# A timetable by single products, tile steps in two halves, and attention rows in pairs

## The chip, the core and the metric

The kernel runs on one core of a Trainium2 chip. Its time is the device time of one execution in microseconds (us), as the median of several runs. Less is better. The core has a matrix engine (TensorE, PE in the profile, with its weight loads as PEld), a vector engine (VectorE, DVE), a scalar engine (ScalarE, ACT), GpSimd (POOL) and SyncE (SP). Each engine works through its own list of instructions in order; the engines wait for each other by semaphores. Transfers are issued from the lists of SP and of POOL and then run on 16 DMA engines that all share.

## The reference

One layer on 2048 tokens of 512 channels: x plus an RWKV attention plus a mixture of experts, both on the normalised x.

```python
x = L0_attn_x                                   # [1, 2048, 512]
xn = _layernorm(x)
x = x + attn(xn) + ffn(xn)

# attn
rvk = einsum('btc,dc->btd', xn, W_rvk)
r, v, k = split(rvk, 3)
y = sigmoid(r) * wkv(time_decay, time_first, k, v)     # scan over time, state (p, q, o) per channel
out = einsum('btc,dc->btd', y, W_out)

# ffn
probs = softmax(einsum('bsh,eh->bse', xn, classifier_w))        # 12 experts, 8 real, 4 that pass x on
idx = top_k(probs + bias, 2); w_full = probs at idx * 1.5
act = silu(xn @ gate_w[e].T) * (xn @ up_w[e].T)                 # INTER = 256
out = sum over e < 8 of w_full[e] * (act @ down_w[e].T) + xn * (sum of w_full[8:])
```

## The kernel before

**Data.** The 2048 tokens are 4 blocks of 512 (`NTB`, `TB`), each of 4 rows of 128 tokens (`NJ`). The channels are 4 groups of 128 (`CC`). A *unit* (b, c) of the attention is one block in one group: three groups of four products (k, v, r; `project`, L259), each group accumulated in one PSUM bank of `ps_mm` and copied by ScalarE to a tile, and then a scan along time (`scan`, L282) on VectorE in four stages, with two exps on ScalarE between the first and the second stage and a reciprocal in the last. A *product* here is one 128x128 by 128x512 matrix product in fp32. When a block's four units are through, its four *attention rows* follow (`attention`, L719): four products with the output weight into one bank, one VectorE add of x's share (L740) onto a row read back from `xs` (`read_xn`, L697), and an accumulating store from POOL into `out` (L743). The normalised x lies in the DRAM tensor `xs`; `out` was filled with x at the start.

**The experts.** Tokens are sorted by expert into 25 *tiles* of 128 places. A tile i takes:

- `gather(i)`: POOL fetches 128 rows of `xs` into xg (two buffers).
- `fetch(i)`, `fetch_down(i)`: SP loads the expert's up weights (gw, 1 MB, three buffers) and down weights (dw, three buffers).
- `flip(i)`: ScalarE copies xg into 16-bit halves (xp, one buffer), SP issues a DMA that transposes them (xq). `unite(i)`: ScalarE joins the halves to xgT. So the transpose is done without TensorE.
- `up(i)`: four products into a bank of `ps_gu`. `activate(i)`: a tanh on ScalarE, two VectorE operations; the result is act.
- `flip_act(i)`, `unite_act(i)`: the same detour for act, by way of ap and aq, one buffer each, to actT. The last two tiles transpose act on TensorE instead (`turn_act`).
- `finish(i)`: two down products into a bank of `ps_o` (two banks), ScalarE scales them into yo (three buffers), and POOL adds them into `out` by an indirect transfer.

**The order.** It is written out by hand (`tc.manual_schedule`): each engine gets its instructions in the order in which the program calls them. Up to unit 3 the program is a fixed sequence. From L770 on it is a *timetable*: a list of entries (time, number of steps, generator), sorted by time and then run through. The times are units of a plan, not measurements. `total` = 44 groups * 3.43 + 25 tiles * 5.2 = 280.9. The 44 groups are 36 of the projections and 8 attention rows of blocks 0 and 1 (`after`, L772). Group m stands at `total * m / groups`, all four products at once. The scan stages of unit u stand at (u - 1) * 19 + 0, 4, 6 and 12. Tile step i stands at 6 + 10.68 i, whole. `read_xn` of a row comes 16 before its group, its add 3 after the group.

`step(i, n)` (L669) calls, in this order: fetch i+2; unite_act i-2; flip_act i-1; up i; activate i; gather i+3; finish i-2; flip i+2; fetch_down i+1; unite i+1. In the last step turn_act and finish of tile i-1 are called too.

After the timetable block 2's rows are read (into places of the four-buffer pool `base`, like rows 0 to 7) and block 3's rows (into one place of the gw weights), and block 2's attention rows follow. Then comes a branch that holds a loop for further tiles, which isn't entered with this data, and the rows of block 3, which add to rows of `out` that are read back (`read_out`).

Rows are numbered i = 4 b + j below. Before the change rows 0 to 7 accumulate in banks of `ps_o`, together with the tiles' down products, and of block 2 every second row in `ps_mm`.

Of the kernel before, what the change touches and what calls it, by code (L numbers as in the profile page):

```python
# [26 lines left out]
F32 = mybir.dt.float32  # L27
# [8 lines left out]
P = 128  # L36
T = 2048
C = 512
CC = C // P
TB = 512  # L40
NTB = T // TB
NJ = TB // P
# [9 lines left out]
TILES = 25  # L52
# [7 lines left out]
def layer(ctx: ExitStack, tc: tile.TileContext, x, w_rvk, w_out, decay, first, cls, ebias, gu, down, out):  # L60
    nc = tc.nc

    def pool(name, bufs, **kw):
        return ctx.enter_context(tc.tile_pool(name=name, bufs=bufs, **kw))
# [18 lines left out]
    ps_tr = pool("ps_tr", 2, space=bass.MemoryType.PSUM)  # L83
# [412 lines left out]
    for m in range(2):  # L496
# [21 lines left out]
        for j in range(NT):  # L518
            k = m * NT + j
# [33 lines left out]
    def gather(i, token=token_i):  # L553

        xg = gathered.tile([P, C], F32, tag="xg", name=f"xg{i}")
        nc.gpsimd.indirect_dma_start(  # L556
            out=xg,
            out_offset=None,
            in_=xs,
            in_offset=bass.IndirectOffsetOnAxis(ap=token[:, i : i + 1], axis=0),  # L560
        )
        st[i] = {"xg": xg}

    def fetch(i, which=which_i):

        e = nc.values_load(
            which[0:1, i : i + 1],
            engines=(SP,),
            min_val=0,
            max_val=E - 1,  # L570
            skip_runtime_bounds_check_because="a sum of E - 1 comparisons",
        )
        w = ewp.tile([P, CC, 2 * INTER], F32, tag="gw", name=f"gw{i}")
        nc.sync.dma_start(w, gu[bass.ds(e, 1)].rearrange("o p c n -> p (o c) n"))
        st[i].update(w=w, e=e)

    def fetch_down(i):
        d = ewp.tile([P, IC, C], F32, tag="dw", name=f"dw{i}")
        nc.sync.dma_start(d, down[bass.ds(st[i]["e"], 1)].rearrange("o p c n -> p (o c) n"))
        st[i]["d"] = d  # L580
# [10 lines left out]
    def flip(i):  # L591

        xp = wk1.tile([P, 2, C], U16, tag="xp", name=f"xp{i}")
        nc.scalar.copy(xp, st[i]["xg"].bitcast(U16).rearrange("p (c h) -> p h c", h=2))  # L594
        xq = ex_p.tile([P, 2 * CC, P], U16, tag="xq", name=f"xq{i}")
        nc.sync.dma_start_transpose(xq, xp.rearrange("p h c -> p (h c)"))
        st[i]["xq"] = xq

    def unite(i):

        xgT = ex_p.tile([P, CC, P], F32, tag="xgT", name=f"xgT{i}")
        nc.scalar.copy(  # L602
            xgT.bitcast(U16).rearrange("p c (t h) -> p c t h", h=2),
            st[i]["xq"].rearrange("p (h c) t -> p c t h", h=2),
        )
        st[i]["xgT"] = xgT

    def up(i, cs):

        if 0 in cs:  # L610
            st[i]["pg"] = ps_gu.tile([P, 2, INTER], F32, tag="gu", name=f"pg{i}")
        pg = st[i]["pg"]
        for c in cs:
            nc.tensor.matmul(  # L614
                pg, st[i]["xgT"][:, c, :], st[i]["w"][:, c, :], start=(c == 0), stop=(c == CC - 1)
            )

    def activate(i):
        pg = st[i]["pg"]

        th = ex_p.tile([P, INTER], F32, tag="th", name=f"th{i}")
        nc.scalar.activation(th, pg[:, 0, :], AF.Tanh, scale=0.5)  # L622
        nc.vector.scalar_tensor_tensor(th, th, 1.0, pg[:, 0, :], ALU.add, ALU.mult)  # L623
        act = ex_p.tile([P, INTER], F32, tag="act", name=f"act{i}")
        nc.vector.tensor_mul(act, th, pg[:, 1, :])
        st[i]["act"] = act

    def turn_act(i):
        pt = ps_tr.tile([P, IC, P], F32, tag="tr", name=f"pa{i}")
        for c in range(IC):  # L630
            nc.tensor.transpose(pt[:, c, :], st[i]["act"][:, c * P : (c + 1) * P], ident)
        actT = ex_p.tile([P, IC, P], F32, tag="actT", name=f"actT{i}")
        nc.scalar.copy(actT, pt)
        st[i]["actT"] = actT

    def flip_act(i):

        ap = wk1.tile([P, 2, INTER], U16, tag="ap", name=f"ap{i}")
        nc.scalar.copy(ap, st[i]["act"].bitcast(U16).rearrange("p (c h) -> p h c", h=2))
        aq = wk1.tile([P, 2 * IC, P], U16, tag="aq", name=f"aq{i}")  # L640
        nc.sync.dma_start_transpose(aq, ap.rearrange("p h c -> p (h c)"))
        st[i]["aq"] = aq

    def unite_act(i):
        actT = ex_p.tile([P, IC, P], F32, tag="actT", name=f"actT{i}")
        nc.scalar.copy(  # L646
            actT.bitcast(U16).rearrange("p c (t h) -> p c t h", h=2),
            st[i]["aq"].rearrange("p (h c) t -> p c t h", h=2),
        )
        st[i]["actT"] = actT  # L650
# [15 lines left out]
        )  # L666
        del st[i]

    def step(i, n):  # L669

        if i + 2 < n:
            fetch(i + 2)
        if i > 1:
            unite_act(i - 2)
        if 0 < i < n - 1:
            flip_act(i - 1)
        up(i, (0, 1))
        if i == n - 1:
            turn_act(i - 1)
        up(i, (2, 3))  # L680
        activate(i)
        if i + 3 < n:
            gather(i + 3)
        if i > 1:
            finish(i - 2)
        if i == n - 1:
            finish(i - 1)
        if i + 2 < n:
            flip(i + 2)
        if 2 <= i + 1 < n:  # L690
            fetch_down(i + 1)
        if i + 1 < n:
            unite(i + 1)

    xrows, orows = {}, {}

    def read_xn(b, js=range(NJ)):  # L697
        if b == NTB - 1:
            t = ewp.tile([P, NJ, C], F32, tag="gw", name=f"xrows{b}")
        for j in js:  # L700
            i = b * NJ + j
            if b == NTB - 1:
                xrows[i] = t[:, j, :]
            else:
                xrows[i] = basep.tile([P, C], F32, tag="base", name=f"xrow{i}")
            nc.sync.dma_start(xrows[i], xs[i * P : (i + 1) * P, :])
# [12 lines left out]
    def attention(b, js=range(NJ)):  # L719

        for j in js:
            i = b * NJ + j
            if j >= 2 if i in orows else b == NTB - 2 and j % 2 == 1:
                po = ps_mm.tile([P, C], F32, tag="mm", name=f"pw{i}")
            else:
                po = ps_o.tile([P, C], F32, tag="o", name=f"pw{i}")
            for c in range(CC):
                nc.tensor.matmul(  # L728
                    po,
                    yT[b][:, c, j * P : (j + 1) * P],  # L730
                    wout_sb[:, c, :],
                    start=(c == 0),
                    stop=(c == CC - 1),
                )
            yield
            if i in orows:
                nc.vector.tensor_add(orows[i], orows[i], po)  # L737
                nc.sync.dma_start(out[i * P : (i + 1) * P, :], orows[i])
            else:
                nc.vector.scalar_tensor_tensor(  # L740
                    xrows[i], xrows[i], zw[:, i : i + 1], po, ALU.mult, ALU.add
                )
                nc.gpsimd.dma_start(out[i * P : (i + 1) * P, :], xrows[i], accum_op=ALU.add)  # L743
            yield


    gather(0)
# [5 lines left out]
    stages = [scan(*u) for u in units]  # L753
# [15 lines left out]

    UNIT = 19.0  # L770
    ahead = [p for p in [project(*u) for u in units[LEAD:]] for _ in range(3)]
    after = {14: (0, 0), 17: (0, 1), 20: (0, 2), 23: (0, 3), 34: (1, 0), 37: (1, 1), 40: (1, 2), 43: (1, 3)}  # L772
    groups = len(ahead) + len(after)
    total = groups * 3.43 + TILES * 5.2
    table = []
    for u in range(1, len(units)):
        for k, at in enumerate((0, 4, 6, 12)):
            table.append(((u - 1) * UNIT + at, 1, stages[u]))
    for m in range(groups):
        at = total * m / groups  # L780
        if m in after:
            b, j = after[m]
            table.append((at - 16, 1, iter([(read_xn, b, [j])])))
            row = attention(b, [j])
            table += [(at, 1, row), (at + 3, 1, row)]
        else:
            table.append((at, CC, ahead.pop(0)))


    spread = (total - 14) / TILES  # L790
    for i in range(TILES):
        table.append((6 + spread * i, 1, iter([(step, i, TILES)])))
    table.append((6 + spread * TILES, 1, iter([(turn_act, TILES - 1)])))
    table.append((9 + spread * TILES, 1, iter([(finish, TILES - 1)])))
    for _, n, work in sorted(table, key=lambda entry: entry[0]):
        for _ in range(n):
            todo = next(work, None)
            if todo:
                todo[0](*todo[1:])
    read_xn(NTB - 2)  # L800
    read_xn(NTB - 1)
    whole(attention(NTB - 2))
    manual.close()

# [69 lines left out]
```

## Time and profile before

| | |
|---|---|
| three runs | 395.91, 396.14, 403.66 us (median 396.14) |
| profiled execution | 394.85 us, span from first to last instruction 393.1 us |
| TensorE clock granted | 1.0 throughout |
| first TensorE instruction | 9.63 us after the span's start |
| DMA | 88.80 MB, mean 226 GB/s |

The page's second part shows 40 slices of the span, each digit the busy share in tenths:

```profile
PE   0999999999999999999999999999999999999995
DVE  5872898997866648677666493976857658857405
ACT  2765112554464555636344644655563455332000
POOL 4002001421041333312233240423331311223300
DMA  8998907465789869879999999799899898843694
```

Of the costliest groups these belong to the tiles and rows of the timetable. Columns: line, engine, operation, output <- inputs, shape, count | busy us, mean ns of one | idle time of the engine just before them, with what ended most of it.

```profile
L614 PE MATMUL pg<-gw,xgT 128*128 128x512 f32 x200 | 90.1, 592 | 0.0
L728 PE MATMUL pw<-wout_sb,yT 128*128 128x512 f32 x128 | 57.0, 594 | 0.9 <-ACT yo L659 0.8
L323 DVE RECIPROCAL den<-den 128x512 f32<-128x512 f32 x16 | 53.5, 3344 | 0.0
L655 PE MATMUL po<-dw,actT 128*128 128x512 f32 x100 | 46.9, 593 | 1.0 <-ACT actT L646 1.0
L602 ACT COPY xgT<-xq 128x1024 uint16<-128x1024 uint16 x25 | 29.0, 1160 | 0.0
```

A busy time is a sum over the records of one group. Idle time counts only on the engine that is the bound; elsewhere it costs nothing by itself.

### The profile page before, as it was taken

The numbers are of one execution on the slowest core, as the hardware profiler recorded it, in microseconds if no ns is written. First come the engines' busy times: TensorE is split into PE (matmuls) and PEld (weight loads), VectorE is DVE, ScalarE is ACT, GpSimd is POOL, SyncE is SP. The second block draws the span as 40 slices with busy tenths as digits, with TensorE's granted clock in tenths as the row PEclk, the third lists the DMA queues.
The fourth block names the chain that finished last, engine by engine and source line by source line (L and its number), as shares of the span: only waits on it lengthen the run. The fifth ranks groups of instructions, "written<-read, shape, count | busy, mean of one in ns | idle before, by whom it ended". The sixth has DMA issues, their size and how long they took to land. (4 is left out here: it accounts for less than half of the span.)

```text
span 393.1 us, 3511 instructions
## 1 busy us (share of the span) xinstructions
PE 374.8 (95%) x994; PEld 169.6 (43%) x994; DVE 271.1 (69%) x397; ACT 170.5 (43%) x278; POOL 98.8 (25%) x130
## 2 busy tenths in 40 slices
PE   0999999999999999999999999999999999999995
PEld 0545445444444434444444444444444444444432
DVE  5872898997866648677666493976857658857405
ACT  2765112554464555636344644655563455332000
POOL 4002001421041333312233240423331311223300
PEclk9999999999999999999999999999999999999999
DMA  8998907465789869879999999799899898843694
GB/s 265 412 392 329 321 28 320 113 177 164 217 220 245 252 155 249 209 227 272 276 260 210 207 261 236 212 263 278 244 262 261 235 208 238 200 64 46 89 258 162
DMA packets 62885, 88.80 MB, mean 226 GB/s; under 512 B 42192, under 2 KB 42320, under 8 KB 59088
## 3 DMA queue, kind: packets, MB, share of 16 engines
q1 hardware_dynamic: 55328, 67.85, 57.1%
q0 software_dynamic: 7536, 20.71, 26.8%
q8 instruction: 8, 0.13, 0.1%
q14 instruction: 13, 0.11, 0.1%
HBM read 63.78 MB, written 19.40 MB: 212 GB/s over the span
## 5 line engine op out<-in xcount | busy, mean ns | idle before, releaser
L614 PE MATMUL pg<-gw,xgT 128*128 128x512 f32 x200 | 90.1, 592 | 0.0
L660 POOL DMA_INDIRECT out_dram<-yo,to_i x25 | 43.3, 1731 | 134.2 <-ACT yo L659 79.7
L265 PE MATMUL pk<-xnT,wrvk 128*128 128x512 f32 x128 | 58.9, 596 | 0.0
L614 PEld LDWEIGHTS pg<-gw,xgT 128*128 128x128 f32 x200 | 37.9, 190 | 47.4 <-issue 45.4
L728 PE MATMUL pw<-wout_sb,yT 128*128 128x512 f32 x128 | 57.0, 594 | 0.9 <-ACT yo L659 0.8
L265 PE MATMUL pr<-xnT,wrvk 128*128 128x512 f32 x128 | 57.7, 592 | 0.0
L265 PE MATMUL pv<-xnT,wrvk 128*128 128x512 f32 x128 | 57.6, 593 | 0.0
L323 DVE RECIPROCAL den<-den 128x512 f32<-128x512 f32 x16 | 53.5, 3344 | 0.0
L309 DVE TENSOR_TENSOR_SCAN sums<-obv,state,a 128x512 f32<-128x512 f32 x16 | 20.5, 1283 | 40.2 <-ACT obv L303 40.2
L655 PE MATMUL po<-dw,actT 128*128 128x512 f32 x100 | 46.9, 593 | 1.0 <-ACT actT L646 1.0
L556 POOL DMA_INDIRECT xg<-xs,token_i x25 | 30.1, 1205 | 43.4 <-DVE empty L543 27.4
L623 DVE SCALAR_TENSOR_TENSOR th<-th,pg 128x256 f32<-128x256 f32 x25 | 10.5, 419 | 41.0 <-ACT th L622 41.0
L728 PEld LDWEIGHTS pw<-wout_sb,yT 128*128 128x128 f32 x128 | 24.0, 190 | 32.0 <-issue 29.6
L265 PEld LDWEIGHTS pv<-xnT,wrvk 128*128 128x128 f32 x128 | 24.2, 190 | 30.1 <-issue 29.9
L265 PEld LDWEIGHTS pr<-xnT,wrvk 128*128 128x128 f32 x128 | 24.2, 190 | 30.1 <-issue 30.1
L265 PEld LDWEIGHTS pk<-xnT,wrvk 128*128 128x128 f32 x128 | 23.7, 190 | 31.2 <-issue 30.6
L659 ACT ACTIVATE yo<-po,wplace 128x512 f32<-128x512 f32 x25 | 17.2, 687 | 35.1 <-PE po L655 35.1
L655 PEld LDWEIGHTS po<-dw,actT 128*128 128x128 f32 x100 | 18.9, 190 | 25.2 <-issue 22.5
L622 ACT ACTIVATE th<-pg 128x256 f32<-128x256 f32 x25 | 9.6, 384 | 45.7 <-PE pg L614 45.6
L602 ACT COPY xgT<-xq 128x1024 uint16<-128x1024 uint16 x25 | 29.0, 1160 | 0.0
L594 ACT COPY xp<-xg 128x1024 uint16<-128x1024 uint16 x25 | 25.9, 1038 | 6.3 <-DMA xq<-xp 3.5
L743 POOL DMA_DIRECT2D out_dram<-xrow x12 | 11.1, 1007 | 56.9 <-DMA out_dram<-yo,to_i 45.5
(151 smaller groups left out, 368.3 us busy)
## 6 DMA issues: line engine op xcount, KB each, us to landing
gw<-in_gu_dram SPq DMA_DIRECT2D x25, 1024.0 KB, 7.5
dw<-in_down_dram SPq DMA_DIRECT2D x25, 512.0 KB, 5.5
x<-in_x_dram SPq DMA_DIRECT2D x16, 256.0 KB, 5.2
xs<-x SPq DMA_DIRECT2D x16, 256.0 KB, 5.0
wrvk<-in_w_rvk_dram SPq DMA_DIRECT2D x3, 1024.0 KB, 7.2
xrow<-xs SPq DMA_DIRECT2D x12, 256.0 KB, 5.2
out_dram<-xrow POOLq DMA_DIRECT2D x12, 256.0 KB, 5.9
wout_sb<-in_w_out_dram SPq DMA_DIRECT2D x1, 1024.0 KB, 10.1
```

Of the source, the lines that this page charges most:

```text
L265: nc.tensor.matmul(ps, wrvk_sb[m][:, k, c * P : (c + 1) * P], xnT[b][:, k, :], start=(k == 0), stop=(k == CC - 1),)
L309: nc.vector.tensor_tensor_scan(sq, bs, a2, s[:, 3:4], ALU.add, ALU.mult)
L323: nc.vector.reciprocal(den, den)
L556: nc.gpsimd.indirect_dma_start(out=xg, out_offset=None, in_=xs, in_offset=bass.IndirectOffsetOnAxis(ap=token[:, i : i + 1], axis=0),)
L594: nc.scalar.copy(xp, st[i]["xg"].bitcast(U16).rearrange("p (c h) -> p h c", h=2))
L602: nc.scalar.copy(xgT.bitcast(U16).rearrange("p c (t h) -> p c t h", h=2), st[i]["xq"].rearrange("p (h c) t -> p c t h", h=2),)
L614: nc.tensor.matmul(pg, st[i]["xgT"][:, c, :], st[i]["w"][:, c, :], start=(c == 0), stop=(c == CC - 1))
L655: nc.tensor.matmul(po, st[i]["actT"][:, c, :], st[i]["d"][:, c, :], start=(c == 0), stop=(c == IC - 1))
L659: nc.scalar.activation(yo, po, AF.Identity, scale=weight[:, i : i + 1])
L660: nc.gpsimd.indirect_dma_start(out=out, out_offset=bass.IndirectOffsetOnAxis(ap=to[:, i : i + 1], axis=0), in_=yo, in_offset=None, compute ...
L728: nc.tensor.matmul(po, yT[b][:, c, j * P : (j + 1) * P], wout_sb[:, c, :], start=(c == 0), stop=(c == CC - 1),)
L743: nc.gpsimd.dma_start(out[i * P : (i + 1) * P, :], xrows[i], accum_op=ALU.add)
```

## The change

The timetable's entries become single calls. A helper `plan(at, what, *args)` adds an entry; a group's four products are planned one by one, `one` = 280.9 / 44 / 4 = 1.596 apart, instead of four at one time, so that other work can stand between them. `attention` yields after each product accordingly, and its add is the fifth call.

`step` is cut into `first_half` (fetch i+2, flip_act i-1, up i, activate i, unite_act i-2, gather i+3) and `second_half` (unite i+1, flip i+2, finish i-2, fetch_down i+1), planned 0.6 of a step later. So unite_act moves behind activate, and unite ahead of flip and finish.

The rows of blocks 0 and 1 stand in pairs of neighbouring groups (14, 15; 20, 21; 34, 35; 42, 43), and both adds of a pair come at one time behind the pair's products. Rows 0 to 5 accumulate in banks of `ps_tr`, row 6 in `ps_o`, row 7 in `ps_mm`. Block 2's rows are read into a weight place (tag gw) as block 3's were, and both reads are entries of the timetable, near its end.

```diff
-    def step(i, n):
+    def first_half(i, n):
         if i + 2 < n:
             fetch(i + 2)
-        if i > 1:
-            unite_act(i - 2)
         if 0 < i < n - 1:
             flip_act(i - 1)
         up(i, (0, 1))
...
         up(i, (2, 3))
         activate(i)
+        if i > 1:
+            unite_act(i - 2)
         if i + 3 < n:
             gather(i + 3)
+
+    def second_half(i, n):
+        if i + 1 < n:
+            unite(i + 1)
+        if i + 2 < n:
+            flip(i + 2)
         if i > 1:
             finish(i - 2)
         if i == n - 1:
             finish(i - 1)
-        if i + 2 < n:
-            flip(i + 2)
         if 2 <= i + 1 < n:
             fetch_down(i + 1)
-        if i + 1 < n:
-            unite(i + 1)
...
     def read_xn(b, js=range(NJ)):
-        if b == NTB - 1:
+        if b >= NTB - 2:
             t = ewp.tile([P, NJ, C], F32, tag="gw", name=f"xrows{b}")
...
-            if j >= 2 if i in orows else b == NTB - 2 and j % 2 == 1:
+            if i < (NTB - 2) * NJ - 2:
+                po = ps_tr.tile([P, C], F32, tag="tr", name=f"pw{i}")
+            elif j >= 2 if i in orows else j % 2 == 1:
                 po = ps_mm.tile([P, C], F32, tag="mm", name=f"pw{i}")
             else:
                 po = ps_o.tile([P, C], F32, tag="o", name=f"pw{i}")
...
-            yield
+                yield
...
-    after = {14: (0, 0), 17: (0, 1), 20: (0, 2), 23: (0, 3), 34: (1, 0), 37: (1, 1), 40: (1, 2), 43: (1, 3)}
+    after = {14: (0, 0), 15: (0, 1), 20: (0, 2), 21: (0, 3), 34: (1, 0), 35: (1, 1), 42: (1, 2), 43: (1, 3)}
+    def plan(at, what, *args):
+        table.append((at, iter([(what, *args)]) if args else what))
...
+    one = total / groups / CC
     for m in range(groups):
-        at = total * m / groups
         if m in after:
             b, j = after[m]
-            table.append((at - 16, 1, iter([(read_xn, b, [j])])))
-            row = attention(b, [j])
-            table += [(at, 1, row), (at + 3, 1, row)]
+            group = attention(b, [j])
+            plan(CC * m * one - 16, read_xn, b, [j])
+            plan(CC * (m + 2 - j % 2) * one + 1, group)
         else:
-            table.append((at, CC, ahead.pop(0)))
+            group = ahead.pop(0)
+        for k in range(CC):
+            plan((CC * m + k) * one, group)
...
     for i in range(TILES):
-        table.append((6 + spread * i, 1, iter([(step, i, TILES)])))
+        plan(6 + spread * i, first_half, i, TILES)
+        plan(6 + spread * (i + 0.6), second_half, i, TILES)
+    plan(8 + spread * (TILES - 1), read_xn, NTB - 2)
+    plan(9 + spread * TILES, read_xn, NTB - 1)
...
-    read_xn(NTB - 2)
-    read_xn(NTB - 1)
     whole(attention(NTB - 2))
```

More of the change, by code (lines that the diff above doesn't have):

```diff
@@ L701, in read_xn @@
             i = b * NJ + j
-            if b == NTB - 1:
+            if b >= NTB - 2:
                 xrows[i] = t[:, j, :]
@@ L743, in attention @@
                 nc.gpsimd.dma_start(out[i * P : (i + 1) * P, :], xrows[i], accum_op=ALU.add)
-            yield
     gather(0)
@@ L775, in layer @@
     table = []
+    def plan(at, what, *args):
+        table.append((at, iter([(what, *args)]) if args else what))
     for u in range(1, len(units)):
-        for k, at in enumerate((0, 4, 6, 12)):
-            table.append(((u - 1) * UNIT + at, 1, stages[u]))
+        for at in (0, 4, 6, 12):
+            plan((u - 1) * UNIT + at, stages[u])
+    one = total / groups / CC
     for m in range(groups):
-        at = total * m / groups
         if m in after:
             b, j = after[m]
-            table.append((at - 16, 1, iter([(read_xn, b, [j])])))
-            row = attention(b, [j])
-            table += [(at, 1, row), (at + 3, 1, row)]
-        else:
-            table.append((at, CC, ahead.pop(0)))
+            group = attention(b, [j])
+            plan(CC * m * one - 16, read_xn, b, [j])
+            plan(CC * (m + 2 - j % 2) * one + 1, group)
+        else:
+            group = ahead.pop(0)
+        for k in range(CC):
+            plan((CC * m + k) * one, group)
     spread = (total - 14) / TILES
     for i in range(TILES):
-        table.append((6 + spread * i, 1, iter([(step, i, TILES)])))
[L793 to L799, printed above, removed]
-    read_xn(NTB - 2)
-    read_xn(NTB - 1)
+        plan(6 + spread * i, first_half, i, TILES)
+        plan(6 + spread * (i + 0.6), second_half, i, TILES)
+    plan(8 + spread * (TILES - 1), read_xn, NTB - 2)
+    plan(9 + spread * TILES, read_xn, NTB - 1)
+    plan(6 + spread * TILES, turn_act, TILES - 1)
+    plan(9 + spread * TILES, finish, TILES - 1)
+    for _, work in sorted(table, key=lambda entry: entry[0]):
+        todo = next(work, None)
+        if todo:
+            todo[0](*todo[1:])
     whole(attention(NTB - 2))
```

## The prediction

> **What bounds the kernel now.** I read the busy shares first, then TensorE's own timeline, then what ScalarE and VectorE did at its gaps, then the DMA table.
>
> ```profile
> PE 374.8 (95%) x994; PEld 169.6 (43%) x994; DVE 271.1 (69%) x397; ACT 170.5 (43%) x278; POOL 98.8 (25%) x130
> ```
>
> TensorE is busy for all but 18 us of the 393.1 us span, and 9.6 us of that is before its first instruction. A long row of the timeline tells more than the share: its starts lie 0.429 us apart (143.02 to 146.02 for eight records of the up product), though a record is drawn 592 ns long. Each 128x512 product of the code is two records, so it costs 0.86 us of TensorE and a group of four 3.43 us. I compared start with start from 66 us on. All follow at 0.429 us except in three places:
>
> ```profile
> 143.02 3.60 PE L614 MATMUL pg<-gw,xgT 128*128 128x512 f32 x8
> 146.77 0.19 ACT L322 COPY state<-sums 128x2 f32<-128x2 f32 x1 [2.78 <-DVE sums L311]
> 146.87 0.67 ACT L646 COPY actT<-aq 128x512 uint16<-128x512 uint16 x1
> 147.59 1.98 PE L655 MATMUL po<-dw,actT 128*128 128x512 f32 x4 [0.98 <-ACT actT L646]
> ...
> 357.57 1.88 PE L655 MATMUL po<-dw,actT 128*128 128x512 f32 x4
> 359.49 0.69 ACT L659 ACTIVATE yo<-po,wplace 128x512 f32<-128x512 f32 x1 [3.48 <-PE po L655]
> 360.23 18.52 PE L728 MATMUL pw<-wout_sb,yT 128*128 128x512 f32 x42 [0.78 <-ACT yo L659]
> ...
> 376.82 0.75 DVE L740 SCALAR_TENSOR_TENSOR xrow<-xrow,zw,pw 128x512 f32<-128x512 f32 x1 [5.24 <-DMA xrow<-xs]
> 377.62 0.30 PEld L728 LDWEIGHTS pw<-wout_sb,yT 128*128 128x128 f32 x2 [0.79 <-DVE xrow L740]
> ```
>
> Columns are start, us, engine, line. (1) At 146.45 the down product of tile 5 was due and began at 147.59: the join `unite_act` stood in ScalarE's queue behind a state copy that waited for a VectorE scan. With 0.10 us before its second record: 1.25 us. (2) At 359.29 row 8 was due and began at 360.23, as it waited for the eviction yo to free a bank: 1.05 us. (3) At the end row 11's add waited 5.24 us for its row and held a bank: 0.22 us; the branch behind it takes another 0.4 us. The sum is **2.9 us, all that any reordering can win behind the start**; after TensorE's end the chain has one add and the last store.
>
> **What the Trainium skill says.** "Perfetto Trace Analysis", Identifying the Most-Contended Engine, says that busy matmul time is no measure of distance to the limit; the trace agrees (592 ns drawn, 429 ns apart), which is why I count starts. "TensorE: Matmul & The Clock Gate", Architectural detail, says that TensorE pulls only weight loads ahead, while ScalarE and VectorE are strict queues; the 146.77 row, a 0.19 us copy that delays a join of another chain, agrees. "Perfetto Trace Analysis", Matmuls, advises to rotate independent groups through different PSUM banks; gap (2) is that advice missed.
>
> **The change, part by part.** I compared the instruction lists of both kernels, engine by engine. No product, copy, scan, gather or transfer is added or removed: only order, tiles and banks change, so TensorE's own work stays and the sum is one of stalls.
>
> *Single products.* A group's four products now alternate with the tiles' products. In the list four products stand between up(i) and the down products of tile i-2, and two or three between these and up(i+1); before, the two followed each other. Cost 0 by itself: 0.86 us a product either way. ps_mm has two banks and a group's copy (0.59 us) has at least 3.43 us.
>
> *Joins ahead.* `unite_act(i-2)` moves behind `activate(i)`: it can start at the end of up(i) plus 0.2 + 0.38 us (tanh), takes 0.67 us, so it is ready some 1.3 us after up(i); its product comes 3.43 us after. Slack 2.1 us where there was none: **gap (1) goes, -1.25 us**. The state copies that block ScalarE now stand before `unite` (1.16 us), whose product is two down products and two or three others later, 3.4 to 4.3 us. One place looks tight: unite(2) follows exps that wait for act of tile 1 and 2.9 us of VectorE (L293 to L300); ready about 5.9 us after up(1) by the rows at 95 to 99 us, wanted after seven products, 6.0 us, less a weight load (0.19). I take +0.1, bounds 0 to +0.5 us.
>
> *What stands behind the moved join.* The one aq tile is overwritten by the transpose of act i-1, which now waits on SP for `unite_act(i-2)`: it is issued some 4.7 us after up(i) begins, not 2 to 3.5. Queued behind it on SP: the transpose of xg (issued some 9 us in, after ScalarE's xp copy), the dw load, the next gw.
>
> ```profile
> gw<-in_gu_dram SPq DMA_DIRECT2D x25, 1024.0 KB, 7.5
> dw<-in_down_dram SPq DMA_DIRECT2D x25, 512.0 KB, 5.5
> xq<-xp SPq DMA_TRANSPOSE x25, 5.1
> aq<-ap SPq DMA_TRANSPOSE x23, 6.5
> ```
>
> Last column: median us from issue to landing. gw and dw have two periods or more. A period is 12 or 13 products, 10.3 to 11.2 us. xq has 8 us until ScalarE wants it and 3.4 more until TensorE does; its longest in the trace is 8.1. aq closes a loop: landing (L), ap copy 0.62, tanh about 0.35, join 0.67, next issue: L + 1.7 us, a period with L = 6.5 being 8.2. The down product stalls for one tile once L passes some 10.7; the longest is 10.3. Cost 0, cover 2.3 us on average; upper bound +2 us for a few late ones in series. Not below 0, since no wait of TensorE's comes earlier through it.
>
> *Finish, flip, gather.* `finish` and its yo move 0.6 of a step later; three yo tiles hold them (one out accumulation takes 6.8 us to land, one a period). `gather(i+3)` gets 1.6 periods before its flip instead of one: 6.5 us to land. POOL's row stores are paired, which saves waits of landings between the kinds; nobody on TensorE waits for POOL within 17 us. 0.
>
> *Rows in pairs.* Rows 0 to 5 accumulate in ps_tr, which the steady part leaves idle, so down products no longer share banks with them; the adds (0.74 us each) come after both. VectorE is 69% busy. 0, as it held up nothing visible. Each xrow load has 14 us.
>
> *Block 2's rows.* They are read into a weight place (one DMA each still) right after the last tile's first half, not from xrow places that came free late: row 11's 5.24 us wait goes, **-0.22 us**. The out rows read after the branch come earlier too, so TensorE stays last.
>
> *Banks at the end, the loss.* Row 6 takes one ps_o bank before po of tile 22 is begun and gives it back only after the last scan, as its add moved behind that. So tile 22 and 23's down products, back to back, share one bank: po 23 must wait for yo 22. Price from gap (2), the same pair: **+1.05 us**. Gap (2) itself goes, as tile 24's product is followed by three of row 7 (2.6 us against 0.9): **-1.05 us**. Row 10 then waits for row 6's add behind the last reciprocal: worked from the end of up(24), exps end at +9.8, scans and sums 5.1, reciprocal and product 4.1, add 0.7: +19.8 us, and row 10 is due at +22.6 us. 0.
>
> Sum: -1.25 + 0.1 - 0.22 + 1.05 - 1.05 = -1.4 us. The profiled execution's span of 393.1 us (394.85 with what lies around it) becomes 391.7 (393.5); the three runs have a median of 396.14, 1.3 above, so the forecast is **394.8**.
>
> **Rivals.** *Whole gain*: if yo 22 finds another bank, or the stall is smaller, -2.3 to -2.5 us: 393.7. For it: row 6 has only one product ahead of po 22. Against: its bank is taken from that first product on. *Nothing*: the DMA engines show no idle share in the middle (below), transposes land late here and there, and four or five stalls of 0.3 to 1 us return what was won: 395.5 to 399.
>
> ```profile
> 210.00:253.00 43.00, 43.00 (x102) 19.08 (x101) 28.23 (x36) 21.16 (x35) 13.81 (x12) 1.00 1.01 241
> 253.00:296.00 43.00, 43.00 (x102) 19.03 (x101) 29.23 (x35) 23.71 (x38) 16.08 (x14) 1.00 1.00 251
> ```
>
> Of these windows the last columns are clock, DMA share and GB/s; TensorE is full all the same. *Slower*: the aq loop becomes the pace. It decides from L = 8.8 us on average (10.5 - 1.7); each us above costs 23 us, so 2% (8 us) is reached at L = 9.15, and at 9.5 the time is 412. For it: 8.8 and 9.8 occur at 230 to 260 us. Against: the median, and that short distances between gw and aq (0.45 us at 166, 187, 289, 321) go. *Not as said*: had the lists kept blocks of four, nothing would change; they don't.
>
> **How the numbers follow.** Forecast 0.55, whole gain 0.12, nothing 0.28, slower 0.05. About 2%, 8 us, can be told from no change here (the three runs span 395.91 to 403.66). Faster by that would need 388.2, below what the gaps allow: 0.01; slower 0.05; within, 0.94. The range 393.0 to 398.6 holds the forecast, the whole gain and most of the third; its low end is the median less 2.9 and a little, its high end the bounds +0.5 and +2 with two more us of late transfers.
>
> **What would show it.** Down product of tile 5 with no idle time before it; tile 23's with about 0.8 us <-ACT yo; row 8 with none; row 11's add with no DMA wait; TensorE's last record near 387.2; SP's aq issues waiting for ACT's actT, and landing within 8.8 us on average. Wrong would be TensorE gaps <-ACT actT or xgT in every step, or an unchanged gap at tile 5.

## The result, and the profile after

| kernel | runs | median, us | least to greatest | span of the profiled run |
|---|---|---|---|---|
| before | 5 | 396.14 | 395.91 to 403.66 | 393.1 |
| after | 5 | 393.05 | 392.30 to 393.24 | 390.9 |

The ratio of after to before is 0.9914, with an interval of 0.9897 to 0.9932: 3.1 us less, where 1.3 less was forecast. The time lies in the forecast range and within 2%. Before has two runs more here than in its table above. (Ratios, here and below, leave out runs over 1.5% above their kernel's fastest; medians and extremes leave out none.)

The page of the kernel after, busy shares and two of TensorE's groups, with the columns explained above:

```profile
PE 374.4 (96%) x994; PEld 169.8 (43%) x994; DVE 270.7 (69%) x397; ACT 169.9 (43%) x278; POOL 97.3 (25%) x130
...
L733 PE MATMUL pw<-wout_sb,yT 128*128 128x512 f32 x128 | 57.3, 593 | 0.1
...
L655 PE MATMUL po<-dw,actT 128*128 128x512 f32 x100 | 47.1, 593 | 0.8 <-ACT yo L659 0.8
```

The busy times hardly differ from before; the idle entries do. The rows' group (L728 before, L733 after) has lost its wait of 0.8 us for yo, and the down group (L655) waits for a yo in place of an actT. TensorE's timeline of after shows where:

```profile
346.41 1.88 PE L655 MATMUL po<-dw,actT 128*128 128x512 f32 x4
349.07 1.98 PE L655 MATMUL po<-dw,actT 128*128 128x512 f32 x4 [0.78 <-ACT yo L659]
350.89 1.88 PE L733 MATMUL pw<-wout_sb,yT 128*128 128x512 f32 x4
```

Tiles 22 and 23 share a bank of `ps_o`, so tile 23's down product waits for tile 22's eviction. And this is the new place of the join `unite_act` (L646) in the tile around 136 us, on ScalarE and TensorE:

```profile
136.10 0.38 ACT L622 ACTIVATE th<-pg 128x256 f32<-128x256 f32 x1 [2.82 <-PE pg L614]
...
136.38 0.66 ACT L646 COPY actT<-aq 128x512 uint16<-128x512 uint16 x1
...
137.61 1.88 PE L265 MATMUL pv<-xnT,wrvk 128*128 128x512 f32 x4
...
139.33 1.88 PE L655 MATMUL po<-dw,actT 128*128 128x512 f32 x4
```

The join ends at 137.04 and its product starts at 139.33, behind two products of k and two of v. Before, this product followed up at once.

Counted start to start as in the prediction, the pauses of TensorE in the two profiled executions are:

| pause | before, us | after, us |
|---|---|---|
| tile 5's down, behind `unite_act` | 1.25 | 0 |
| up of tile 2 (the "tight place") | 0 | 0.07 |
| a bank of `ps_o`, behind yo | 1.05 (row 8) | 1.05 (tile 23) |
| row 11's row, late | 0.22 | 0 |
| the branch | 0.39 | 0.39 |

From 65.7 us in before, 65.4 in after, to behind the branch it is 313.17 us before and 311.75 after: 1.42 less, and the sum forecast was 1.4 less. After's start is a further 0.31 shorter and its end from the branch on 0.47. The start varies by itself, as is seen below. The end doesn't: from TensorE's last start to the end of the span it is 5.04 to 5.23 us in the profiles of before and its variants and 4.60 to 4.63 in those of after and its variants. In the two profiles the 0.47 lies behind TensorE's last start; the prediction has no term for it, and its cause was not looked for. So in its pauses the two *profiles* agree with the prediction; the two *medians* differ by 1.7 us more than its sum. Of that the experiments treat.

### The profile page after: what moved, and what is told of

Read it like the earlier page. It is cut to its first block, busy times and chain, and to the rows that moved or that the text cites. A ratio compares the mean times of both kernels' runs of the same rounds, so it can differ in the third digit from the quotient of the medians.

```text
span 390.9 us, 3494 instructions
## 1 busy us (share of the span) xinstructions
PE 374.4 (96%) x994; PEld 169.8 (43%) x994; DVE 270.7 (69%) x397; ACT 169.9 (43%) x278; POOL 97.3 (25%) x130
## 5 line engine op out<-in xcount | busy, mean ns | idle before, releaser
L660 POOL DMA_INDIRECT out_dram<-yo,to_i x25 | 44.7, 1789 | 156.7 <-ACT yo L659 75.9
L265 PE MATMUL pk<-xnT,wrvk 128*128 128x512 f32 x128 | 60.5, 596 | 0.0
L265 PE MATMUL pv<-xnT,wrvk 128*128 128x512 f32 x128 | 59.7, 593 | 0.0
L265 PE MATMUL pr<-xnT,wrvk 128*128 128x512 f32 x128 | 59.5, 592 | 0.0
L733 PE MATMUL pw<-wout_sb,yT 128*128 128x512 f32 x128 | 57.3, 593 | 0.1
L655 PE MATMUL po<-dw,actT 128*128 128x512 f32 x100 | 47.1, 593 | 0.8 <-ACT yo L659 0.8
L556 POOL DMA_INDIRECT xg<-xs,token_i x25 | 26.8, 1072 | 48.8 <-DVE empty L543 27.5
L733 PEld LDWEIGHTS pw<-wout_sb,yT 128*128 128x128 f32 x128 | 24.2, 190 | 30.6 <-issue 30.4
L655 PEld LDWEIGHTS po<-dw,actT 128*128 128x128 f32 x100 | 18.9, 190 | 25.0 <-issue 22.5
L602 ACT COPY xgT<-xq 128x1024 uint16<-128x1024 uint16 x25 | 28.9, 1158 | 0.0
L230 PE MATMUL pt<-ident,x 128*128 128x128 f32 x64 | 12.5, 326 | 11.0 <-DVE x L220 9.3
```

Of the source, the lines that this page charges most:

```text
L230: nc.tensor.transpose(pt[:, j * P : (j + 1) * P], xt[b * NJ + j][:, c * P : (c + 1) * P], ident)
L265: nc.tensor.matmul(ps, wrvk_sb[m][:, k, c * P : (c + 1) * P], xnT[b][:, k, :], start=(k == 0), stop=(k == CC - 1),)
L556: nc.gpsimd.indirect_dma_start(out=xg, out_offset=None, in_=xs, in_offset=bass.IndirectOffsetOnAxis(ap=token[:, i : i + 1], axis=0),)
L602: nc.scalar.copy(xgT.bitcast(U16).rearrange("p c (t h) -> p c t h", h=2), st[i]["xq"].rearrange("p (h c) t -> p c t h", h=2),)
L655: nc.tensor.matmul(po, st[i]["actT"][:, c, :], st[i]["d"][:, c, :], start=(c == 0), stop=(c == IC - 1))
L660: nc.gpsimd.indirect_dma_start(out=out, out_offset=bass.IndirectOffsetOnAxis(ap=to[:, i : i + 1], axis=0), in_=yo, in_offset=None, compute ...
```

## The experiments

Each kernel ran beside the kernel before on one chip. The medians of before there were 397.53 us for the first four, 397.15 for the next four, 396.74 for the three after these, 396.77 for b_halves and b_both1 to b_both3, and 396.96 for the last two.

### Where do other executions of before lose time?

Theory A: other executions pause at other thin places in the timetable. Theory B: they differ in the start and the end. First the kernel before as it is, b1 in 14 runs and b2 in one.

> The kernel before, unchanged, profiled again. Its first profile had TensorE gaps of 2.9 us from 66 us on and a span of 393.1 us, 1.3 below what its median leaves for a span. Theory A (thin joins): other executions lose more at joins of the kind seen at tile 5, which one profile happened to miss; this profile shows the 1.05 us at row 8 again and 1.5 to 4 us of gaps before actT or xgT, at other tiles too. Theory B (ends): the same three gaps, and the rest lies before TensorE's first instruction (9.6 us) or behind its last (some 4 us). Against itself: ratio 1.00.

> The kernel before once more, for the spread between profiles. Theory A: gaps in the timetable differ from b1's in place and sum, and the span follows their sum. Theory B: same gaps, the span follows the start and the end.

b1: median 397.03 (394.02 to 401.19). b2: 394.29. b2's profile has the pauses at tile 5 and row 8 and the branch, and no other. The profiled execution of b1 took 400.4 us (span 398.6) and has a pause that no profile so far had. ScalarE and TensorE of b1:

```profile
234.75 1.04 ACT L594 COPY xp<-xg 128x1024 uint16<-128x1024 uint16 x1 [6.76 <-DMA xg<-xs,token_i]
235.70 1.15 ACT L602 COPY xgT<-xq 128x1024 uint16<-128x1024 uint16 x1
...
236.91 5.31 PE L614 MATMUL pg<-gw,xgT 128*128 128x512 f32 x8 [2.77 <-ACT xgT L602]
```

ScalarE stood 6.76 us at the copy xp, the head of `flip(i+2)`, for rows that had not landed. The join `unite(i+1)` (L602) is queued behind it, and up waits for that join. The gather itself was late because of POOL's list:

```profile
223.46 0.97 POOL L743 DMA_DIRECT2D out_dram<-xrow  x1 [8.22 <-DMA out_dram<-yo,to_i]
224.73 1.80 POOL L556 DMA_INDIRECT xg<-xs,token_i  x1 [0.30 <-ACT ap L639]
```

A row's accumulating store waited 8.22 us for a tile's accumulation to land, and the gather stood behind it. The pause of 2.93 us drew 1.71 us of slow products behind it: 4.64 us, beside the familiar ones. A is right in kind (the loss is in the timetable), but the join was another than I had thought of.

Beside these ran two variants of after. row6 gives row 6 a bank of `ps_tr` too:

```diff
-            if i < (NTB - 2) * NJ - 2:
+            if i < (NTB - 2) * NJ - 1:
```

> The changed kernel with row 6 in a bank of ps_tr, so that the down products of tiles 22 and 23 have a ps_o bank each. If the 1.05 us at tile 23 is lost to the bank that row 6 holds: 1.0 us less than the changed kernel, 392.0 us, ratio to before 0.989 to 0.990, and the gap before po 23 gone. Rival: TensorE's end is not what sets the end, or the wait moves to row 8 or 10: 393.0 us, no difference.

391.99 (391.28 to 392.21, 6 runs), ratio 0.9848 (0.9807 to 0.9889). The pause at tile 23 is gone and no other came. It is the fastest kernel of this study.

a_uact puts `unite_act(i-2)` back to the head of the first half:

```diff
+        if i > 1:
+            unite_act(i - 2)
         if 0 < i < n - 1:
             flip_act(i - 1)
...
         activate(i)
-        if i > 1:
-            unite_act(i - 2)
```

> The changed kernel with unite_act back in its old place ahead of flip_act at the head of the first half; the down products stay in the second half. If the later finish alone made the slack (the join has 3.43 us of up products and four single products more): same time as the changed kernel, 393 us, no gap at tile 5. If the join's place behind activate made it: gaps at state copies come back, 394.3 us or more.

393.15 (392.19 to 394.44, 6 runs), ratio 0.9881 (0.9838 to 0.9924), as after, and no pause at tile 5. So it is not the join's new place that covers it: `finish` standing later is enough.

### One cause: the late gather, or something else?

Theory C: what b1 showed is the whole remainder. Theory D: it comes from POOL's rows or from whole groups. Theory E: the earlier gather is the cure, not the order of join and flip. b_join changes before:

```diff
+        if i + 1 < n:
+            unite(i + 1)
         if i + 2 < n:
             flip(i + 2)
         if 2 <= i + 1 < n:
             fetch_down(i + 1)
-        if i + 1 < n:
-            unite(i + 1)
```

> The kernel before with one edit: in step, unite(i+1) is issued ahead of flip(i+2) and not as the last thing; the rest stays. Theory C (late gather held in front of the join): before's loss beyond the three fixed gaps comes in executions in which a gather lands late, because ScalarE's copy of xgT for the next tile stands behind its copy of xp, which waits for that gather. Then this kernel keeps the two fixed gaps (1.25 at tile 5, 1.05 at row 8) and loses the rest: median 394.0 to 395.0, no time above 396, no pause of TensorE over 0.5 us released by ScalarE's xgT. Rival D (the scatter comes from POOL's accumulating rows or from whole groups, not from the join's place): median within 0.5 of before on the same chip, 396 to 397.5, with the same scatter.

397.22 (393.86 to 403.49, 14 runs), ratio 0.9969 (0.9937 to 1.0000): C missed by 2.6 us. But the profile of b_join (an execution of 399.72) has no pause for xgT. It has another, near the end, while row 11's add held a bank. SP, POOL, VectorE and TensorE of b_join:

```profile
336.44 38.21 SPq L706 DMA_DIRECT2D xrow<-xs  x5
...
370.25 3.58 POOL L743 DMA_DIRECT2D out_dram<-xrow  x4 [3.69 <-DMA out_dram<-yo,to_i]
...
380.05 0.75 DVE L740 SCALAR_TENSOR_TENSOR xrow<-xrow,zw,pw 128x512 f32<-128x512 f32 x1 [9.20 <-DMA xrow<-xs]
...
380.86 1.12 PE L728 MATMUL pw<-wout_sb,yT 128*128 128x512 f32 x2 [3.92 <-DVE xrow L740]
```

The reads of rows 7 to 11 took from 336.44 to 374.65 to issue: row 11's needs the buffer of row 7, whose store stood on POOL until the last tile's accumulation had landed, at 370.25. In the first profile of before the same stores were issued at 367.67 and the wait cost 0.22 us. Here, 2.6 us later, TensorE lost 4.08 us and 1.77 more in slow products.

This execution does not stand alone. Six of b_join's 14 runs, it among them, took 399.72 to 403.49 us, with a granted clock of 0.993 or less over the run; of before's 51 runs beside them three had so low a clock. The other eight have a median of 395.40, where before's other 48 have 397.11. So the edit looks worth some 1.7 us, hidden by a second pause. That the other five runs had this pause isn't shown, nor why it came oftener than in before.

The other three are variants of after: a_flip (flip ahead of unite), a_gather (`gather(i+3)` in the second half, between unite and flip) and a_groups (a group's products at one time).

```diff
 a_flip
-        if i + 1 < n:
-            unite(i + 1)
         if i + 2 < n:
             flip(i + 2)
+        if i + 1 < n:
+            unite(i + 1)
 a_groups
-            plan((CC * m + k) * one, group)
+            plan(CC * m * one, group)
```

> The changed kernel with flip(i+2) issued ahead of unite(i+1) in the second half; the gather stays in the first half, so it has 1.6 tile periods and not about one before the flip. Theory C in its strong form (the order of join and flip alone counts): some executions lose 1 to 4 us again, median 394 to 396. Theory C in its weak form (either the order or the earlier gather is enough): as the changed kernel, 392.5 to 393.5. Rival D: as the changed kernel, 392.5 to 393.5. So this run tells the two forms apart, and b_join tells C from D.

394.49 (393.45 to 396.29, 22 runs), ratio 0.9943 (0.9922 to 0.9964): 1.4 above after's 393.05. Two pauses <- ACT xgT are in its profile, at tiles 1 and 2, 0.46 and 1.02 us with their second records, so 1.48 us. ScalarE at the second:

```profile
99.52 1.03 ACT L594 COPY xp<-xg 128x1024 uint16<-128x1024 uint16 x1
100.45 1.16 ACT L602 COPY xgT<-xq 128x1024 uint16<-128x1024 uint16 x1
```

The time is what strong C names, but not by a late gather: the copy xp did not wait here. It took its own 1.03 us in front of the join, at a place where the join has no time to spare.

> The changed kernel with gather(i+3) moved from the first half to the second, between unite(i+1) and flip(i+2): it then has one tile period (some 8.6 us) before its flip, as in the kernel before, while the join stays ahead of the flip. Theory C: the flip waits longer but nothing that TensorE needs at once stands behind it: 392.8 to 393.8, at most 0.7 above the changed kernel. Rival E (the earlier gather is what takes the loss away): 394.5 to 397, with pauses at up of a tile.

393.02 (392.48 to 393.28, 6 runs), ratio 0.9903 (0.9867 to 0.9939), as after. E falls: the gather's longer lead isn't needed, as long as the join stands ahead of the flip.

> The changed kernel with the four products of a projection or row given one and the same time in the timetable, so that groups stay whole and everything else is placed around them. Theory C: single products by themselves bring nothing, 392.7 to 393.7, at most 0.5 above the changed kernel; a gap may move by some tenths. Rival D (single products make the cover of the joins): 394.5 or more, with pauses of 0.4 us and over at down or up of a tile that the changed kernel has not.

395.61 (394.72 to 397.95, 22 runs), ratio 0.9971 (0.9953 to 0.9988): 2.6 above after. C missed; D has the median, with smaller pauses than it named. Its TensorE and ScalarE, at the first of six like places:

```profile
108.66 1.88 PE L655 MATMUL po<-dw,actT 128*128 128x512 f32 x4
110.55 2.84 PE L614 MATMUL pg<-gw,xgT 128*128 128x512 f32 x6
...
108.86 0.60 ACT L276 ACTIVATE r<-pr 128x512 f32<-128x512 f32 x1 [2.39 <-PE pr L265]
109.35 1.15 ACT L602 COPY xgT<-xq 128x1024 uint16<-128x1024 uint16 x1
```

With whole groups only the two down products stand between the second half and the next up: 1.72 us for a join that needs 1.15 and has r's copy ahead of it. Six pauses of 0.28 us make 1.70, and a second wait for a bank at row 8 makes 1.05: 2.75 in sum. So halves of steps need single products (or another filler) between them.

### Two late transfers

Theory F: row 11's read is what varies. b_place is before with block 2's rows in a weight place; b_both has b_join's edit too; a_base is after with this part undone.

```diff
 b_place, b_both (in both lines of read_xn)
-        if b == NTB - 1:
+        if b >= NTB - 2:
 a_base: the reverse, and
-    plan(8 + spread * (TILES - 1), read_xn, NTB - 2)
+    plan(8.5 + spread * TILES, read_xn, NTB - 2)
```

> The kernel before with one part of the change: block 2's rows are read into a weight place, as block 3's are, so that the read of row 11 no longer waits for an accumulating write on GpSimd to land and free a buffer. Theory F (row 11's read is what varies: it came 0 us late in one execution of the kernel before, 0.1 and 0.4 in two others, and 4.1 us with 1.7 us of slower products behind it in the execution of b_join): median 394.0 to 395.0, few times above 396; the two fixed gaps stay. Theory C (the late gather in front of the join makes most of it): median 396 to 397.5, scatter as before. Theory D (neither; whole groups make it): 396 to 397.5.

396.43 (393.84 to 398.89, 22 runs), ratio 1.0021 (1.0000 to 1.0042). F missed its median by 1.4. Its profile shows nothing at the rows, and the pause of b1 again, at the same tile: TensorE 1.70 us <- ACT xgT at 234.84, ScalarE before it, at the copy xp at 232.68, 5.51 us <- DMA xg. Yet the longest times are gone and the middle stays: none of the 22 runs took over 399 us, where 14 of before's 59 did.

> The kernel before with both edits: unite(i+1) ahead of flip(i+2) in step, and block 2's rows in a weight place. If both late transfers count, this is steady and b_place is not: 393.8 to 394.6 with less than 2 us between the least and the greatest time. If only row 11's read counts (F), it equals b_place within 0.4. Under D both stay at 396 to 397.5.

395.12 (393.89 to 401.27, 22 runs), ratio 0.9969 (0.9942 to 0.9997). The forecast for two causes missed, by 0.5 in the median and by far in the steadiness. The median is 1.6 below before's; b_place alone had moved it by 0.3, b_join, on another chip, by less. By the ratios b_both and b_join can't be told apart; that both causes count rests on the profiles and on a_base.

> The changed kernel with this one part undone: block 2's rows are read into the buffers of the earlier rows again, behind the last tile's second half, and so row 11's read waits for an accumulating write again. Theory F: the changed kernel's times spread as those of before do, 393 to 400 with a median of 394 to 396.5, and TensorE pauses ahead of a row among 12 to 15 behind VectorE's wait for the read. Theory C or D: 392.8 to 393.5, as the changed kernel.

398.20 (394.55 to 400.37, 22 runs), ratio 1.0031 (0.9998 to 1.0063): this one part undone costs the kernel after 5.15 us of median, more than F had said; C and D are excluded. Waits of TensorE of a_base:

```profile
PE pw L733 <- DVE xrow L745: 4.1, 1, 4.1
```

and its POOL:

```profile
367.67 3.61 POOL L748 DMA_DIRECT2D out_dram<-xrow  x4 [3.81 <-DMA out_dram<-yo,to_i]
379.86 1.74 POOL L748 DMA_DIRECT2D out_dram<-xrow  x2 [8.58 <-DVE xrow L745]
```

The pause was 4.24 us and the slow products behind it cost 2.36. The part that the prediction had at 0.22 us is what after needs most. After's pairs make it worse than in before: rows 6 and 7 are stored together behind the last scan, so the reads of both row 10 and row 11 come late. So a_base is not quite the old arrangement; it shows what the old reads would cost in the new timetable.

### What is left: the down product too close to its join

b_both still lies above its fixed pauses now and then. Theory H: down products that follow `unite_act` at once, behind a late aq. Rival K: single products or pairs of rows are needed. Three more executions of b_both (their expectations are alike) and a kernel with halves, b_halves: b_both with the step cut behind gather, and the rest of it, finish first, 0.6 of a period later.

> The kernel of b_both once more, one look. Theory H: where TensorE pauses beyond 146 us (tile 5) and 359 us (row 8), it does so ahead of a tile's down, released by ScalarE's unite_act (L646) behind a late transpose aq; 394 to 396, or about 400 with slower products behind the pause. Rival K: pauses ahead of a row or of up instead.

> The kernel of b_both, a second look. Theory H: pauses beyond those at tile 5 and row 8 stand ahead of a tile's down, released by ScalarE's unite_act behind a late transpose. Rival K: ahead of a row or of up instead.

> The kernel of b_both, a third look. Theory H: pauses beyond those at tile 5 and row 8 stand ahead of a tile's down, released by ScalarE's unite_act behind a late transpose. Rival K: ahead of a row or of up instead.

396.77, 394.34 and 395.08 us. Beyond the fixed pauses they have 1.66, 0.14 and 0; the profile of b_both itself has 0.31, as the second at a down product behind a join that waited for aq. The first in ScalarE and TensorE of b_both1:

```profile
270.91 0.67 ACT L646 COPY actT<-aq 128x512 uint16<-128x512 uint16 x1 [3.48 <-DMA aq<-ap]
...
271.63 1.98 PE L655 MATMUL po<-dw,actT 128*128 128x512 f32 x4 [1.39 <-ACT actT L646]
```

As H has it: a transpose landed late, 13.2 us after its issue, and its product came straight behind up. (The third, with no such pause, started TensorE 0.84 us later than the second: 10.07 against 9.23 us. The start varies by itself.) But four of b_both's 22 runs took 399.29 to 401.27 us, as none of b_place's did, and none of the four was profiled: what they lost isn't shown.

> b_both with step cut in two as in the changed kernel: up, activate and gather at the step's time, finish, unite, flip and fetch_down 0.6 of a tile period later; unite_act stays at the head, groups stay whole, rows stay single. Theory H (the remainder lies in down products that follow their join unite_act at once, so finish 0.6 of a period later covers it): the gap at tile 5's down goes, the one at row 8 or at a down stays: 392.7 to 393.7, no time above 395. Rival K (single products or pairs of rows cover it): at tile 5 1.25 less, and a tail as b_both has, with times above 398.

408.36 (407.74 to 414.10, 6 runs), ratio 1.0349 (1.0288 to 1.0410). Both missed. Seven times TensorE waited, as here, with ScalarE's part:

```profile
108.43 1.88 PE L655 MATMUL po<-dw,actT 128*128 128x512 f32 x4
112.13 3.27 PE L614 MATMUL pg<-gw,xgT 128*128 128x512 f32 x7 [1.82 <-ACT xgT L602]
...
110.34 0.69 ACT L659 ACTIVATE yo<-po,wplace 128x512 f32<-128x512 f32 x1 [1.12 <-PE po L655]
110.93 1.14 ACT L602 COPY xgT<-xq 128x1024 uint16<-128x1024 uint16 x1
```

With finish ahead of unite, the join stands behind yo, which waits for the down product, and up comes right behind that product. 7 x 2.09 = 14.6 us, less tile 5's 1.25: 13.4, and 395.12 + 13.4 = 408.5. It couldn't decide between H and K, so b_fin moves the down products alone, a group away from up:

```diff
     def step(i, n):
...
-        if i > 1:
-            finish(i - 2)
-        if i == n - 1:
-            finish(i - 1)
...
+    def down_half(i, n):
+        if i > 1:
+            finish(i - 2)
+        if i == n - 1:
+            finish(i - 1)
         if 2 <= i + 1 < n:
             fetch_down(i + 1)
...
         table.append((6 + spread * i, 1, iter([(step, i, TILES)])))
+        table.append((6 + spread * i + 6.39, 1, iter([(down_half, i, TILES)])))
```

> b_both with finish (and fetch_down behind it) moved out of step to an entry of its own 6.39 of plan time later, so that one whole group stands between up and the down products; groups stay whole, rows single, unite and flip where b_both has them. Theory H (a down product too close behind its join unite_act is the remainder): no pause at tile 5 and none behind a late aq; the pause at row 8 or a like one at a bank may stay: median 392.7 to 394.0, none above 396. Rival K (single products or pairs of rows are needed): tile 5's 1.25 goes but the times still spread up to 398 or more, median 394.5 to 396, with pauses ahead of up or of a row.

> The changed kernel itself, beside b_fin and on the same chip. Both theories: 392.3 to 393.3 with no time above 394; its profile shows the one pause at the down product of tile 23 (1.05) and the branch.

b_fin: 393.49 (392.51 to 395.95, 15 runs), ratio 0.9929 (0.9902 to 0.9955). a_again: 392.87 (392.34 to 393.29, 6 runs), ratio 0.9895 (0.9849 to 0.9942). b_fin's profile has one pause ahead of the branch, row 8's bank of 1.05. ScalarE waited three times for aq, 2.9 us in sum, with landings of up to 11.2 us, and TensorE not once. H holds: three small edits of before, with whole groups and single rows, come within 0.6 us of the kernel after. Its greatest time is 2.7 above after's, and what the rest of the scatter is was not looked at.

## Why the prediction was right in its sum and wrong in its size

**Joins ahead, -1.25: right, for one of several places.** Tile 5's pause went. But it was only the place at which a down product behind up hurts in every execution; in others a late aq hurts elsewhere (1.66 us in b_both1). b_fin against b_both, with before at 397.0 and 396.7 beside them, is worth 1.6: tile 5's 1.25 and 0.4 more. a_uact shows that the later finish does it, not the join's place, to which I had given the credit. The tight place, unite(2), cost 0.07; I had 0.1.

**"Single products, cost 0 by itself": right, and too short.** They cost nothing, but a_groups shows that the halves would lose 2.6 us without them. I had not said what covers the joins if groups stay whole.

**What stands behind the moved join, 0: right.** aq landed in 5.6 us at the median and 9.0 at most; the loop never became the pace.

**"Finish, flip, gather: 0": this step failed.** I asked how long the gather has, and found 6.5 us against a period. I did not ask what is queued behind its consumer: before, the next tile's join. One late gather cost 4.6 us in b1 and 1.8 in b_place. With unite ahead of flip such a gather no longer holds the join: b_both, with this edit, is 1.3 below b_place, without it, on the same chip. In after the same order is worth 1.4 by a_flip, there for the copy's own time.

**"Block 2's rows, -0.22": mis-sized.** The mechanism was right, the size that of one execution. With its slow products the same wait cost 0 in b2, 0.54 in b1, 5.86 in b_join; and undoing the part in after (a_base) cost 5.15.

**Banks at the end: right to the hundredth.** Tile 23's wait came at 1.05 and row 8's went at 1.05. row6 shows that the new one was needless: 0.9 below a_again, 1.16 below a_uact, which ran on its chip.

**The term of the sum that was wrong** is the last one: "three runs have a median of 396.14, 1.3 above, so the forecast is 394.8". It carried the distance between the profiled execution and the median over to the changed kernel, as if the chip and not the kernel had made it. It was made in the kernel: by two transfers, now and then late, in front of work that TensorE needs at once, and by thin joins. The change moves all of these out of the way, so its times lie within 1 us of each other (392.30 to 393.24). Had I taken the 1.3 for pauses that the change removes too, the forecast would have been the profiled execution less the sum, 394.85 - 1.4 = 393.5; with the end shorter by 0.47 it is 393.0. For the same reason "2.9 us, all that any reordering can win behind the start" was wrong: b1 had those pauses and 4.6 us more.

Of the rivals, "Whole gain" came nearest in time (393.7) by luck: its reason, a free bank for tile 23, did not come. "Nothing" and "Slower" did not come either. "Not as said" is excluded by the products of k and v that stand between up and down at 136 us; tile 5 alone wouldn't do it, as its pause is gone in a_groups too.

Open: why b_join has so many long runs, what b_both's four longest lost, and the 0.6 us between b_fin and after. Of these 0.4 lie in the end (5.04 against 4.60 us behind TensorE's last start); from its first start to its last TensorE took 376.9 us in b_fin's profile and 377.0 in a_again's. So single products and pairs of rows show no gain of their own there, beyond the cover that the halves need. Pairs of rows were not tried alone.

## What to carry to other kernels

Before you take a gap list from one profile as the list of what can be won, look at how the kernel's times spread: a median 1.3 us above the profiled run, with a range of 8, is itself a finding, and a reordering may remove it. For each queue, ask of every instruction that waits for a DMA: what stands behind it that the bounding engine needs soon? Put the join of data that has landed ahead of the copy that may have to wait, and read a row into a place that no unfinished store has to free. When a step is cut in pieces, check that something stands between the pieces on the bounding engine, for in b_halves, where nothing did, a join of 1.15 us behind an eviction cost 2.09 us at each of seven tiles.

## What was not expected of the hardware

A long pause of TensorE costs more than itself. Behind pauses of 2.93, 4.08 and 4.24 us (b1, b_join, a_base) the products' starts lay mostly 0.85 us apart, where 0.43 is normal, for some 3 to 5 us, which added 1.71, 1.77 and 2.36 us. The granted clock reads 0.50 there and 1.00 on both sides: for 3.41 us in b1 and b_join and for 6.83 in a_base. The drop came at the pause's end in b1 (236.76 us), 1.2 us behind it in b_join (382.08 against 380.86) and 2.0 before it in a_base (378.35 against 380.32). Behind pauses of 1.56 to 2.0 us (b_both1, b_place and seven times in b_halves) only the usual 0.10 us followed, and the clock there reads 1.00. The Trainium skill, "TensorE: Matmul & The Clock Gate", HAM oscillation — how this bites in real kernels, says that gaps over some 3.4 us throw the array back to half its clock; the doubled distance of starts agrees, and here 2.93 us was enough.

The landing time of an accumulating transfer reaches far: a row's add that was done by 210.93 in b1 had its store issued only at 223.46, behind a tile's accumulation issued at 212.96, and with it the gather.
